# Convolution-fed attention: nine batches of eight key blocks instead of twelve of six

## The chip, the cores and the metric

The kernel runs on one core of one Trainium2 chip. The metric is device time in microseconds (us), the median of the runs shown. TensorE is called PE, its weight loads PEld, VectorE DVE, ScalarE ACT, GpSimd POOL, SyncE SP.

## The reference

The input x has shape (4, 384, 48, 48): four images, 384 channels, 2304 positions. All is fp32.

```
local  = depthwise_conv7x7(x) with batch norm
x_norm = layernorm(x over channels)
q, k, v = split(x_norm @ qkv_w.T + qkv_b)         # 8 heads of 48
q      = q + layernorm(local over channels)
attn   = softmax(q k^T * 48**-0.5)                # 2304 x 2304 per head
out    = x + (attn v) @ proj_w.T + proj_b
```

## The kernel before

An image has five groups of queries, of 8, 10, 10, 10 and 10 rows of 48 positions (`ROWS`), so 384 columns in the first group and 480 in the others. Four images make 20 groups, `t` = 0 to 19; `g` is the group's place in its image. Between images lies a stage that makes keys, values and raw queries out of the normalized x (`from_x`, six pieces), and adds up the output of the image before.

Within a group the attention loops over four pairs of heads and 18 blocks of 128 keys, 72 blocks in all. They are cut into 12 batches ("slots") of `BATCH` = 6 blocks. For one block `score` issues six matmuls (three terms for each of two heads, the heads on different halves of the array's rows) into a PSUM tile of two banks, one for each head, and one exponential on ACT over both heads (L1113), which writes a `pt` tile (four buffers). `score_batch` does this for six blocks. `weigh_batch` then multiplies the six `pt` tiles with the values (L1120), adding up in one more PSUM tile, `o`. So PE alternates: 36 score matmuls, then 12 weighing matmuls (each fp32 one is two records in the profile). PSUM is one ring of four tiles of two banks, tag `r`; the scores, the sums `o` and all other matmuls take their tiles from it in turn. A tile is free again when the engine that reads it is done.

A pair's sums come in three parts. ACT copies the first into its place in `ao` (L1007) and the others into `part_o` (L997, two buffers); DVE adds these (`sums_add`, L1016). The fourth pair has its own tile `aot`.

The order of each engine's work is written out by hand; each engine takes its instructions in that order. In slot s come: the scores; the first half of the slot's share of convolution on DVE (`convolve`, L340); `sums_add`; the weighing; the second half of the convolution. The share of each half is planned from `spare`, a hand-made table of DVE time left over. Around these lie steps that belong to the next group: the norm of its local convolution, in steps that are seven slots long, and, in late groups of an image, the norm of a piece of the next image's x. Groups 0 to 3 make the means of the query norm on PE (`early`). Groups 4 to 19 add up on DVE, send sums through DRAM by SP (`out`), and take a root of a small tile on ACT (`few_root`). `norm_slots` and `X_SLOTS` give the slots of these steps. `query_end` finishes the next group's queries; `high_queries` (ACT, L968) and `low_queries` (DVE, L973, and six DMAs on SP) split them into two parts and stack them in a `qs` tile for each head pair. `gather_tails` gathers by eight DMAs on SP the fourth pair's rows into `qt`. `load_keys` loads a third of a pair's keys (18 blocks are three thirds) from DRAM by POOL's queue into one of three `ks` buffers. `divide`, `hold` and `fetch` work on the output of the group before.

Of the kernel before, what the change touches and what calls it, by code (L numbers as in the profile page):

```python
# [16 lines left out]
P = 128  # L17
# [8 lines left out]
BATCH = 6  # L26
NSLOT = 12
X_SLOTS = 4, 7
X_LATER = 3
OUT_SLOT = 7  # L30
# [18 lines left out]
def unshifted_pass(  # L49
# [47 lines left out]
    ps = ctx.enter_context(tc.tile_pool(name="ps", bufs=4, space=bass.MemoryType.PSUM))  # L97
# [8 lines left out]
    def two_banks(name="r"):  # L106
        return ps.tile([P, 2, 512], F32, tag="r", name=name)
# [62 lines left out]
    third = BATCH * P  # L170
# [68 lines left out]
    def pack():  # L239
        m = two_banks()[:, 0, 0 : CC * (T0 + 1)].rearrange("p (c v) -> p c v", c=CC)  # L240
        for c in range(CC):
            mine = [pair for pair in pairs if pair[0] == c]
            for pair in mine:
                nc.tensor.matmul(
                    m[:, c, :],
                    lhsT=packing[:, pairs.index(pair), :],
                    rhs=natural[:, pair[1], :],
                    start=pair == mine[0],
                    stop=pair == mine[-1],
                )  # L250
        nc.scalar.copy(vec, m)
# [126 lines left out]
    def taps_out():  # L378
        m = two_banks()[:, 0, 0 : 4 * T0].rearrange("p (q v) -> p q v", q=4)
# [25 lines left out]
    def products():  # L405
        total = two_banks()[:, 0, : columns_of(1)]
# [21 lines left out]
    def norm_slots(t):  # L428
        return (8 - (t > 0), None) if t + 1 < NA else (5, 8)

    def spare(t, s, half):
        b, g = divmod(t, NA)
        first, second = norm_slots(t)
        time = 3.6 - (0.0 if half else 0.6) - (0.6 if half and s % 3 == 1 else 0.0)
        if b + 1 < B and g >= begins(b + 1):
            time -= {(2, 1): 2.3, (4, 1): 2.2, (5, 1): 2.3, (7, 0): 0.4, (8, 0): 2.6}.get(
                (s, half), 0.0
            )
        if g:
            time -= {(2, 0): 0.7, (7, 1): 1.4}.get((s, half), 0.0)  # L440
        if t + 1 < NA:
            if t:
                time -= {
                    (first, 0): 1.3,
                    (first + 1, 0): 1.4,
                    (first + 1, 1): 1.3,
                    (first + 2, 1): 4.3,
                    (first + 3, 1): 0.6,
                }.get((s, half), 0.0)
            else:  # L450
                time -= {(first + 1, 0): 1.4, (first + 2, 0): 4.3, (first + 2, 1): 0.6}.get(
                    (s, half), 0.0
                )
        elif g < NA - 1:
            time -= {
                (3, 1): 2.3, (5, 0): 1.2, (5, 1): 2.2, (6, 1): 2.3, (8, 0): 0.4, (8, 1): 1.5,
                (9, 0): 4.5,
            }.get((s, half), 0.0)
        return max(0.3, time) * columns_of(t) / G
# [21 lines left out]
    for t in range(NT):  # L481
# [3 lines left out]
        points += [("slot", t, s, h) for s in range(NSLOT) for h in range(2)]  # L485
        room += [spare(t, s, h) for s in range(NSLOT) for h in range(2)]
# [4 lines left out]
    for t in range(1, NT):  # L491
        last = ("slot", t - 1, norm_slots(t - 1)[0] - (t >= NA), t < NA) if t % NA else ("kv", t, 4, 0)
# [41 lines left out]
    class Norm:  # L534
# [41 lines left out]
        def mean_by_chunk(self, src, m=None):  # L576
            self.m = two_banks()[:, 0, : self.n] if m is None else m
            project(self.m, lambda c: mean_w, lambda c: src[:, c, :])
# [5 lines left out]
        def mean_kept(self, src):  # L584

            m = two_banks()[:, 0, : self.n]
# [3 lines left out]
        def mean_of_sum(self):  # L590

            m = two_banks()[:, 0, : self.n]
# [3 lines left out]
        def mean_in_place(self):  # L596

            self.m = two_banks()[:, 0, : self.n]
            nc.tensor.matmul(self.m, lhsT=mean_w, rhs=self.buf[:, 0, :], start=True, stop=True)

        def mean_of(self, src, at):

            self.m = two_banks()[:, 0, :G]
# [92 lines left out]
    def gather_tails(dst, src):  # L696

        for i, c in enumerate((*range(CC), 0)):
# [69 lines left out]
    def from_x(b, g, before=None, ao=None):  # L768
# [22 lines left out]
        def key(u, r):  # L791
# [7 lines left out]
            else:  # L799
                k = work.tile([P, 2, GM], HALF, tag="pt", name=f"k{b}_{g}_{u}", bufs=4)[:, :, :G]  # L800
# [33 lines left out]
        while todo:  # L834
            r = two_banks()
            steps = [f(i, r[:, j, :]) for j, (f, i) in enumerate(todo[:2])]
# [27 lines left out]
    def shift_rows():  # L864
        r = two_banks()
        for c in range(CC):
            for i in range(3):
                nc.tensor.matmul(
                    r[of_row(i), 0, :C],
# [5 lines left out]
        rows.update((i, r[of_row(i), 0, :C]) for i in range(3))  # L875
# [12 lines left out]
    def columns():  # L888

        r, r2 = two_banks(), two_banks()  # L890
        m = {1: r[:, 0, 0:CC], 2: r[:, 1, 0:CC], 0: r2[:, 0, 0:CC]}
# [9 lines left out]
        return m, r2[:, 1, :G]  # L901
# [22 lines left out]
    def output_bias():  # L924

        m = two_banks()[:, 0, 0:CC]
# [17 lines left out]
    def query_end(t, at_once=False):  # L944
# [3 lines left out]
        q3 = work.tile([P, GM], F32, tag="qt", name=f"qt{t}", bufs=1)[:, : columns_of(t)]  # L948
        queries[t] = q, q3
# [36 lines left out]
    ended = []  # L986
    parts_of = deque()

    def sums_out():

        if not ended:
            return
        t, p, i, sums = ended.pop()
        n = columns_of(t)
        if i:
            part = work.tile([P, GM], F32, tag="part_o", name=f"o{t}_{p}_{i}")[:, :n]
            nc.scalar.copy(part[0 : 64 + HA], sums[0 : 64 + HA, 0, :n])  # L997
            parts_of.append((t, p, i, part))
            return
        if p == 0:  # L1000
            ao = work.tile([P, CC, GM], F32, tag="ao", name=f"ao{t}")[:, :, :n]
            ao3 = work.tile([P, GM], F32, tag="aot", name=f"aot{t}", bufs=1)[:, :n]
            den = dram.tile([NH, n], F32, tag=f"den{n}", name=f"den{t}")
            outputs[t] = ao, ao3, den
        ao, ao3, den = outputs[t]
        dst = ao[:, p, :] if p < CC else ao3
        nc.scalar.copy(dst[0 : 64 + HA], sums[0 : 64 + HA, 0, :n])  # L1007

    def sums_add():
# [3 lines left out]
        t, p, i, part = parts_of.popleft()  # L1013
        ao, ao3, den = outputs[t]
        dst = (ao[:, p, :] if p < CC else ao3)[0 : 64 + HA]
        nc.vector.tensor_add(dst, dst, part[0 : 64 + HA])  # L1016
        if i < KB // BATCH - 1:
# [77 lines left out]
    jobs, between = deque(), deque()  # L1095
    weighing = deque()

    def score(t, p, kb):
        ks, qs = stacks[t // NA, p, kb // BATCH], stacked[t, p]
        at = slice(kb % BATCH * P, (kb % BATCH + 1) * P)  # L1100
        n = columns_of(t)
        r = two_banks()
        for i, (w, m) in enumerate(((0, 0), (0, 1), (1, 2))):
            for j, rows in enumerate(halves):
                nc.tensor.matmul(  # L1105
                    r[:, j, :n],
# [5 lines left out]
        pt = work.tile([P, 2, GM], F32, tag="pt", name="pt", bufs=4)[:, :, :n]  # L1112
        nc.scalar.activation(pt, r[:, :, :n], AF.Exp, scale=SCALE)  # L1113
        weighing.append((t, p, kb, pt))

    def weigh(i, sums):
        t, p, kb, pt = weighing.popleft()
        for j in range(2):
            first = (kb % NB * NH + 2 * p + j) * HA
            nc.tensor.matmul(  # L1120
                sums[halves[j], 0, : columns_of(t)],
                lhsT=values[t // NA, kb // NB][:, first : first + 64],
                rhs=pt[:, j, :],
                start=i == 0,
                stop=i == BATCH - 1,
            )

    def score_batch(t, s):
        p, k0 = s // (KB // BATCH), s % (KB // BATCH) * BATCH
        for kb in range(k0, k0 + BATCH):  # L1130
            score(t, p, kb)
            if between:
                between.popleft()()

    def weigh_batch(t, s):
        p, i = s // (KB // BATCH), s % (KB // BATCH)
# [4 lines left out]
        sums = two_banks("o")  # L1141
        for n in range(BATCH):
            weigh(n, sums)
        ended.append((t, p, i, sums))
        sums_out()
# [14 lines left out]
    def warm(n):  # L1160
        m = two_banks()[:, 0, 0:P]
# [31 lines left out]
    m, bank = columns()  # L1193
    convolve_first(10)
    norm = Norm(xn[0, 1])
    norm.mean_by_chunk(norm.src, bank)
# [88 lines left out]

    for t in range(NT):
# [73 lines left out]
        first, second = norm_slots(t)  # L1360
        for s in range(NSLOT):
            pair, part = divmod(s, KB // BATCH)
            score_batch(t, s)
            if part == 0 and pair < NP - 1:
                high_queries(t, pair + 1)
            if s == 0:
                gather_tails(*reversed(queries[t]))
            if s == 0 and g == 0:
                keep_stack(b, 2)
            if (s or g) and (s < NSLOT - 2 or g < NA - 1):  # L1370
                load_keys(b, s + 2, nc.scalar if g == 0 and s < 3 else nc.gpsimd)
            if s == 2 and g:
                rb = divide(t - 1)
            if s == 0 and coming:
                load_x(b + 1, g - begins(b + 1))
            if s == NSLOT - 4 and g == NA - 1:
# [4 lines left out]
                else:  # L1381
                    places = [("acc", 3)] * 3 + [("sq", 2)] * 2 + [("qs", 5)]
                    aos = []
                    for i in range(NG):
                        load_residual(b, i, *places[i])
                        aos.append(fetch(b, i) if i < NG - 1 else outputs[t][0])
            if coming and s == X_SLOTS[1] + 1:
                norm_x.scale(norm_x.few_newton())
            if following and s == second + 1:
                local_end(t + 1, norm.few_newton())  # L1390
                query_end(t + 1, True)
            if coming and s == X_SLOTS[0] + 1:
                jobs.extend(norm_x.square_jobs())
            if following and s == first + 1:
                jobs.extend(norm.square_jobs())
            if coming and s == X_SLOTS[1]:
                norm_x.few_variance()
            if following and s == second:
                norm.few_variance()
# [3 lines left out]
            else:  # L1403
                convolve("slot", t, s, 0)
            sums_add()
            if early and s == first + 1:
# [7 lines left out]
            if coming and s == X_SLOTS[1]:  # L1414
                norm_x.few_root()
            if following and s == second:
                norm.few_root()
# [3 lines left out]
            weigh_batch(t, s)  # L1421
            if early and s == first:
# [5 lines left out]
            if early and s == first + (2 if t == 0 else 3):  # L1428
                low_queries(t + 1, 0)
            convolve("slot", t, s, 1)  # L1430
            if t and early and s == first + 2:
# [589 lines left out]
```

## Time and profile before

| | |
|---|---|
| median of 3 runs | 2739.45 us (2737.72 to 2742.43) |
| the profiled execution | 2739.04 us |
| its span, first to last instruction | 2737.2 us, granted clock 0.997 |
| PE busy | 2714.7 us (99%) |
| DVE busy | 2314.8 us (85%) |
| ACT busy | 1671.1 us (61%) |
| POOL busy | 603.9 us (22%) |

The rows of a group name the line, the engine, the operation, what is written and read, and the shape; then come the number of instructions, the time in which at least one of them ran, the mean length of one in ns, and the idle time of the engine just before them with what ended it. Two matmuls that run side by side each have a record, so the mean length times the number is more than the busy time. In a timeline a row begins with its start and its length in us.

### The profile page before, as it was taken

To read this page: it belongs to the slowest core of one execution; us is meant where nothing else is said; L and a number is where in the kernel's file an instruction comes from. 1 tells how busy PE (TensorE), PEld (TensorE's weight loads), DVE (VectorE), ACT (ScalarE), POOL (GpSimd) and SP (SyncE) were. 2 spreads that over 40 slices of the span, in tenths; PEclk is the share of its full clock that TensorE was granted. 3 is DMA by queue.
4 is the path that set the end of the run, shared out by engine and by line. 5 is a ranking of instruction groups with operands and counts; after the bars stand their busy time and mean duration, and the time that the engine had idled before them with its cause. 6 is when DMAs were issued, how large, how long until landed. Compare 5 with 4: busy or idle time off the path is not lost.

```text
span 2737.2 us, 46047 instructions
## 1 busy us (share of the span) xinstructions
PE 2714.7 (99%) x16438; PEld 1536.6 (56%) x16438; DVE 2314.8 (85%) x4038; ACT 1671.1 (61%) x2317; POOL 603.9 (22%) x1077
## 2 busy tenths in 40 slices
PE   8999999999999999999999999999999999999999
PEld 5565555555556555555555655555555565555555
DVE  7999999989999999989889999889888998986212
ACT  4356777777325777777622677777752377776762
POOL 5541101102453111011155211111225511110110
PEclk9999999999999999999999999999999999999999
DMA  8354544446465545354555553545635544444442
GB/s 164 85 143 136 142 115 129 124 136 182 101 160 154 139 120 146 115 152 124 143 140 138 166 147 110 142 126 141 152 105 158 147 140 133 139 132 132 139 150 68
DMA packets 160223, 370.46 MB, mean 135 GB/s; under 512 B 58672, under 2 KB 107472, under 8 KB 159984
## 3 DMA queue, kind: packets, MB, share of 16 engines
q0 software_dynamic: 71424, 279.04, 35.6%
q1 hardware_dynamic: 83248, 78.33, 12.6%
q10 hardware_dynamic: 5312, 10.06, 1.1%
q8 instruction: 132, 2.16, 0.3%
q14 instruction: 107, 0.88, 0.1%
HBM read 258.14 MB, written 64.14 MB: 118 GB/s over the span
## 4 chain that ended last, share of the span: by engine, by line
PE 90%; DVE 5%; DMA 4%; ACT 0%; issue 0%; SPq 0%; POOL 0%; DVEq 0%; POOLq 0%; ACTq 0%
PE o L1120 42%; PE r L1105 34%; PE r L694 13%; DVE acc L340 2%; DMA parts<-part 1%; DMA staged<-in_qkv_wT_dram 1%; DVE k L804 0%; DMA slab<-in_x_dram 0%; PE r L415 0%; DMA four<-parts 0%; DVE xn L689 0%; DMA wide<-k 0%; DMA xn<-in_x_dram 0%; DMA out_dram<-xr 0%; DVE xr L1086 0%
## 5 line engine op out<-in xcount | busy, mean ns | idle before, releaser
L340 DVE SCALAR_TENSOR_TENSOR acc<-slab,vec,acc 128x470 f32<-128x470 f32 (+10 forms) x2832 | 1658.1, 658 | 2.0 <-ACT acc L303 2.0
L1113 ACT ACTIVATE pt<-r 128x960 f32<-128x960 f32 (+1 forms) x1440 | 1248.6, 943 | 246.4 <-PE o L1120 151.8
L1120 PE MATMUL o<-pt,v 128*64 128x480 f32 (+1 forms) x5760 | 1166.2, 554 | 0.4 <-ACT pt L1113 0.4
L1105 PE MATMUL r<-qs,ks 64*128 64x480 f32 (+1 forms) x8640 | 967.0, 373 | 4.8 <-ACT xn L818 3.0
L1105 PEld LDWEIGHTS r<-qs,ks 64*128 64x128 f32 x8640 | 785.2, 184 | 268.2 <-issue 171.6
L1120 PEld LDWEIGHTS o<-pt,v 128*64 128x64 f32 x5760 | 392.5, 137 | 659.9 <-issue 566.5
L766 POOL DMA_DIRECT2D ks<-wide x220 | 160.0, 727 | 1369.7 <-PE r L1105 1310.0
L694 PE MATMUL r<-xn,w_qk 128*128 128x384 f32 x864 | 284.7, 487 | 0.0
L997 ACT COPY o<-o 113x480 f32<-113x480 f32 (+1 forms) x160 | 87.1, 544 | 277.3 <-PE o L1120 276.7
L694 PEld LDWEIGHTS r<-xn,w_qk 128*128 128x128 f32 x864 | 164.4, 191 | 115.3 <-issue 1.8
L694 PE MATMUL r<-w_v,xn 128*128 128x384 f32 x432 | 145.3, 489 | 2.8 <-DVE xn L689 1.4
L788 ACT COPY v<-r 128x384 f32<-128x384 f32 x72 | 32.0, 479 | 183.3 <-PE r L694 183.3
L1016 DVE TENSOR_TENSOR ao<-ao,o 113x480 f32<-113x480 f32 (+1 forms) x120 | 75.9, 633 | 73.9 <-ACT o L997 73.9
L694 PEld LDWEIGHTS r<-w_v,xn 128*128 128x128 f32 x432 | 81.1, 190 | 62.6 <-DVE xn L689 3.8
L973 DVE TENSOR_TENSOR qs<-xn,qs 128x480 fp32r<-128x480 f32 (+1 forms) x60 | 38.1, 635 | 63.8 <-ACT qs L968 63.8
L751 POOL DMA_DIRECT2D wide<-k x144 | 72.4, 505 | 78.3 <-ACT k L801 64.2
L694 PE MATMUL r<-af,w_o 128*128 128x384 f32 (+1 forms) x270 | 85.2, 470 | 0.0
L1007 ACT COPY ao<-o 113x480 f32<-113x480 f32 (+1 forms) x60 | 32.6, 544 | 72.1 <-PE o L1120 72.1
L1016 DVE TENSOR_TENSOR aot<-aot,o 113x480 f32<-113x480 f32 (+1 forms) x40 | 25.4, 634 | 56.9 <-ACT o L997 56.9
L818 ACT ACTIVATE xn<-r,qkb 128x384 f32<-128x384 f32 x72 | 39.6, 576 | 50.8 <-PE r L694 47.6
L1086 DVE SCALAR_TENSOR_TENSOR xr<-r,pb,xr 128x384 f32<-128x384 f32 (+2 forms) x72 | 42.0, 611 | 33.2 <-PE r L694 26.0
L694 PEld LDWEIGHTS r<-af,w_o 128*128 128x128 f32 x270 | 51.3, 190 | 31.9
(148 smaller groups left out, 1354.9 us busy)
## 6 DMA issues: line engine op xcount, KB each, us to landing
ks<-wide POOLq DMA_DIRECT2D x220, 768.0 KB, 4.9
qs<-qs SPq DMA_DIRECT2D x352, 60.0 KB
slab<-in_x_dram POOLq DMA_DIRECT2D x24, 432.0 KB, 7.2
wide<-k POOLq DMA_DIRECT2D x96, 96.0 KB, 2.2
wide<-ks POOLq DMA_DIRECT2D x12, 768.0 KB, 5.3
xr<-in_x_dram POOLq DMA_DIRECT2D x16, 576.0 KB, 5.6
rb<-rden SPq DMA_DIRECT2D x32, 270.0 KB
held<-ao POOLq DMA_DIRECT2D x12, 720.0 KB, 3.9
```

The costliest lines, as they stand in the source:

```text
L340: nc.vector.scalar_tensor_tensor(dst, src, weight, dst, ALU.mult, ALU.add)
L694: nc.tensor.matmul(dst, lhsT=weights(c), rhs=src(c), start=c == 0, stop=c == CC - 1)
L751: nc.gpsimd.dma_start(out=last[16 * u : 16 * u + 16, 0], in_=k[r : r + 16, 0])
L766: queue.dma_start(out=place_keys(b, p, i), in_=wide[b, p][:, :, at])
L818: nc.scalar.activation(src[:, i, :], q[:, :G], AF.Identity, bias=qkb[:, 0, i : i + 1])
L973: nc.vector.tensor_sub(qs[:, 1, :], query_of(t, p), qs[:, 0, :])
L997: nc.scalar.copy(part[0 : 64 + HA], sums[0 : 64 + HA, 0, :n])
L1016: nc.vector.tensor_add(dst, dst, part[0 : 64 + HA])
L1086: nc.vector.scalar_tensor_tensor(xr[:, co, :], m, pb[:, co : co + 1], xr[:, co, :], ALU.add, ALU.add)
L1105: nc.tensor.matmul(r[:, j, :n], lhsT=ks[rows, w, at], rhs=qs[rows, m, :], start=i == 0, stop=i == 2,)
L1113: nc.scalar.activation(pt, r[:, :, :n], AF.Exp, scale=SCALE)
L1120: nc.tensor.matmul(sums[halves[j], 0, : columns_of(t)], lhsT=values[t // NA, kb // NB][:, first : first + 64], rhs=pt[:, j, :], start=i == ...
```

## The change

Groups 4 to 19 have nine batches of eight blocks; groups 0 to 3 keep twelve of six. A batch of eight can cross from one head pair to the next; then its weighing has two sums. PSUM is a ring of eight single banks, tag `r`: a block takes one for each head, the sums take one. Each head has its own exponential. `pt` has five buffers instead of four (the key tiles that share the tag also); `part_o` has one instead of two; the fourth pair's output uses the tag of the gathered tails (`qt`) instead of its own. The steps of the norms, of the division and of the queries have new places, given as (slot, stage) in tables: stage 0 lies between the scores and the first half of the convolution, 1 before the weighing, 2 before the second half of the convolution, 3 after it. Some ACT steps (`few_root`, and `high_queries` of the next group) are put in a queue `in_gap`, which is emptied among the scores, after the block that is fourth from the batch's end (the fifth of eight). The other pairs' queries are split in slots 0, 2, 4 instead of 0, 3, 6. `gather_tails` is issued after `sums_add` instead of before it. The planner's table `spare` is new for nine slots.

```diff
-BATCH = 6
-NSLOT = 12
-X_SLOTS = 4, 7
+THIRD = 6
+PLACES_9 = {
+    "x_sum": (1, 3), "x_centre": (3, 1), "x_squares": (3, 1), "x_sum_squares": (3, 3),
+    "x_variance": (4, 3), "x_root": (4, 3), "x_scale": (5, 3),
+    "divide": (1, 1), "multiply": (5, 1), "fetch": (6, 0),
+    "q_sum": (2, 3), "q_centre": (4, 1), "q_squares": (4, 1), "q_sum_squares": (4, 3),
+    "q_variance": (5, 3), "q_root": (5, 3), "q_end": (6, 1), "q_high": (6, 3), "q_low": (7, 3),
+}
+HIGHS = {12: (0, 3, 6), 9: (0, 2, 4)}
...
-    ps = ctx.enter_context(tc.tile_pool(name="ps", bufs=4, space=bass.MemoryType.PSUM))
+    ps = ctx.enter_context(tc.tile_pool(name="ps", bufs=8, space=bass.MemoryType.PSUM))
...
-    def two_banks(name="r"):
-        return ps.tile([P, 2, 512], F32, tag="r", name=name)
+    def bank(name="r"):
+        return ps.tile([P, 512], F32, tag="r", name=name)
...
+    def few_slots(t):
+        return t + 1 >= NA
+
+    def n_slots(t):
+        return 9 if few_slots(t) else 12
+
+    def batch(t):
+        return NP * KB // n_slots(t)
...
+        if few_slots(t):
+            time = 4.7 if half else 4.0
...
     def score(t, p, kb):
...
-        r = two_banks()
+        r = bank(), bank()
         for i, (w, m) in enumerate(((0, 0), (0, 1), (1, 2))):
             for j, rows in enumerate(halves):
                 nc.tensor.matmul(
-                    r[:, j, :n],
+                    r[j][:, :n],
...
-        pt = work.tile([P, 2, GM], F32, tag="pt", name="pt", bufs=4)[:, :, :n]
-        nc.scalar.activation(pt, r[:, :, :n], AF.Exp, scale=SCALE)
+        pt = work.tile([P, 2, GM], F32, tag="pt", name="pt", bufs=5)[:, :, :n]
+        for j in range(2):
+            nc.scalar.activation(pt[:, j, :], r[j][:, :n], AF.Exp, scale=SCALE)
         weighing.append((t, p, kb, pt))
...
     def score_batch(t, s):
-        p, k0 = s // (KB // BATCH), s % (KB // BATCH) * BATCH
-        for kb in range(k0, k0 + BATCH):
-            score(t, p, kb)
+        n = batch(t)
+        for i in range(n):
+            score(t, *divmod(s * n + i, KB))
             if between:
                 between.popleft()()
+            while i == n - 4 and in_gap:
+                in_gap.popleft()()
 
     def weigh_batch(t, s):
...
-        sums = two_banks("o")
-        for n in range(BATCH):
-            weigh(n, sums)
-        ended.append((t, p, i, sums))
-        sums_out()
+        i = s * n
+        while i < (s + 1) * n:
+            p, first = divmod(i, KB)
+            many = min(KB - first, (s + 1) * n - i)
+            sums = bank("o")
+            for k in range(many):
+                weigh(k == 0, k == many - 1, sums)
+            sums_out(t, p, first == 0, first + many == KB, sums)
+            i += many
...
+        for s in range(n_slots(t)):
             score_batch(t, s)
...
+            if few_slots(t):
+                n = batch(t)
+                if t == NA - 1 and s == 0:
+                    load_keys(b, 2)
+                for i in range(s * n // THIRD, (s + 1) * n // THIRD):
+                    if i + 3 < NP * 3 or g < NA - 1:
+                        load_keys(b, i + 3)
...
             sums_add()
+            if s == 0:
+                gather_tails(t)
```

## The prediction

> **What bounds the kernel now.** First the page's busy times, to see which engine has no slack.
>
> ```profile
> PE 2714.7 (99%) x16438; PEld 1536.6 (56%) x16438; DVE 2314.8 (85%) x4038; ACT 1671.1 (61%) x2317; POOL 603.9 (22%) x1077
> ```
>
> TensorE (PE) is busy 2714.7 of 2737.2 us, so what saves no PE time and adds no PE wait is worth nothing. Next, groups of instructions with shapes kept apart: the score matmuls (L1105), the weighing matmuls (L1120) and the exponentials (L1113).
>
> ```profile
> L1113 ACT ACTIVATE pt<-r 128x960 f32<-128x960 f32 x1152 | 1035.4, 974 | 192.8 <-PE o L1120 127.2 <-PE r L1105 65.1
> L1120 PE MATMUL o<-pt,v 128*64 128x480 f32 x4608 | 969.8, 570 | 0.0
> L1105 PE MATMUL r<-qs,ks 64*128 64x480 f32 x6912 | 800.2, 381 | 0.9 <-DMA qs<-qs 0.9
> L1113 ACT ACTIVATE pt<-r 128x768 f32<-128x768 f32 x288 | 213.2, 815 | 53.6 <-PE o L1120 24.6 <-DMA wide<-k 15.3 <-PE r L1105 13.3
> ```
>
> Before the matmuls PE was idle 0.9 us in all: today it waits for nobody in the attention. Third, the timeline of one batch on PE, then on ScalarE (ACT).
>
> ```profile
> 1003.76 4.17 PE L1105 MATMUL r<-qs,ks 64*128 64x480 f32 x36
> 1007.86 5.05 PE L1120 MATMUL o<-pt,v 128*64 128x480 f32 x24
> 1012.84 1.34 PE L1105 MATMUL r<-qs,ks 64*128 64x480 f32 x10
> ```
>
> ```profile
> 1003.88 0.56 ACT L997 COPY o<-o 113x480 f32<-113x480 f32 x1 [2.13 <-PE o L1120]
> 1004.78 3.56 ACT L1113 ACTIVATE pt<-r 128x960 f32<-128x960 f32 x4 [0.34 <-PE r L1105]
> 1008.99 1.83 ACT L1113 ACTIVATE pt<-r 128x960 f32<-128x960 f32 x2 [0.66 <-PE o L1120]
> ```
>
> A batch lasts 1012.84 - 1003.76 = 9.08 us. In its single records matmuls start in pairs (two heads side by side): score pairs every 0.217 us, but 0.320 from the first to the second; 0.312 from the last score pair to the first weighing pair; weighing pairs every 0.4025, but 0.453 after the first and 0.503 from the last to the next batch's scores. So 9.08 = 6 x (3 x 0.217 + 2 x 0.4025) + fixed cost, and each batch has a **fixed cost** of 0.103 + 0.095 + 0.050 + 0.100 = 0.348 us. Tiles of 384 columns (steps 0.175 and 0.323) give 0.350.
>
> On ACT four exponentials run back to back (3.56 = 3 x 0.863 + 0.97); the fifth waits for the first weighing, to free one of four `pt` buffers. ACT then idles 1.5 to 2 us per batch: it is not the bound, but it is the pacemaker of PSUM's release.
>
> **Fewer batches (gain).** Sixteen of the 20 groups go from 12 batches to 9: 16 x 3 = 48 batches fewer, 48 x 0.348 = 16.7 us off the path. Matmuls stay the same in number. Where a batch crosses a head pair (batches 2, 4, 6) the weighing changes its bank once; a change of bank between score blocks costs nothing (0.217 on both sides), so 0.
>
> **Eight scores at a stretch (loss).** With eight banks, two per block, the scores of block k need the banks of block k-4: blocks 4, 5, 6, 7 wait for the exponentials of 0, 1, 2, 3. Before, a batch had only blocks 4 and 5, and exponentials 0 and 1 were done early. Now ACT, slower per block than PE (0.85 against 0.651), is raced for two blocks more.
>
> The price of a 480-column exponential is not in the trace. The single records give the spacing back to back: 0.850 for 960 elements, 0.690 for 768, hence 0.833 ns per element plus 0.050 us, so 0.450 per head at 480, **0.900 per block against 0.850**. The nearest rows at 480: the PSUM copies of L997 (0.560 long; a record outlasts its spacing by 0.121, so 0.439) and the SBUF casts of L968 (0.593, spaced 0.480). I take 0.450, from the same operation, source and line; ends 0.439 and 0.480.
>
> The Trainium skill, ScalarE: Activation LUTs, What ACT_TABLE_LOAD costs, says that an ACTIVATE with immediates takes 186 ns + 0.833 ns per element and that neighbours overlap by 93 ns. By that rule a block would go from 893 to 986 ns; this trace's 850 at 960 elements is below it. With 0.493 per head the sum below would be about +71 us, the span about 2808.
>
> Now the race, from the batch's first score. Exponential 0 starts at 1.017 (the trace: 1004.78 - 1003.76); the first spacing is 0.019 longer; a record outlasts its spacing by 0.121; PE starts 0.053 after ACT's end where it really waited (an exponential ended at 245.829 us, the score load started at 245.880). After that wait the next step was 0.278 instead of 0.175: 0.103 of restart, as the load is otherwise issued a pair ahead. Bounds of the restart: 0 (a load 0.10 late cost 0.04) and 0.103; I take 0.103.
> - Block 6 would start at 0.103 + 18 x 0.217 = 4.010; its banks and restart allow 1.017 + 0.019 + 6 x 0.450 + 0.121 + 0.053 + 0.103 = 4.013. No wait.
> - Block 7 would start at 0.103 + 21 x 0.217 = 4.661; allowed 4.913. **Wait 0.25 us.**
> - 384 columns: exponential 0 at 0.895 (median of those batches), head spacing 0.370. Block 7 would start at 3.78, allowed 1.017 + 0.019 - 0.122 + 8 x 0.370 + 0.277 = 4.15. Wait 0.37.
>
> Per group of 480: 9 x 0.25 - 3 x 0.348 = +1.2 us, 13 groups: +15.7. Per group of 384 (the first of images 1 to 3): 9 x 0.37 - 1.05 = +2.3, three: +6.9. **Sum +22.6 us.** With the cheap ends (0.439, restart 0) the same lines give -0.5 x 13 + 0.6 x 3 = -4.7; with 0.480 and restart 0.103, +57.
>
> **The rest of the batch.** The fifth `pt` lets exponential 4 run among the scores; 5, 6, 7 wait for weighings 0, 1, 2 and end about 9.6 us into a batch of 12.2, when weighing 7 needs its own at 11.3: no wait. ACT's 2.6 us up to the next batch hide the query copies (0.59) or squares (1.5). The four first groups keep batches of six, never reach blocks 6 and 7, and pay the dearer exponential on ACT's slack: 0. Without that slack it would be 0.05 x 72 = 3.6 us a group.
>
> **Norm steps and queues.** DVE has the same number of kinds of work, 85% busy, 102.32 of 108.90 us in a full group (below). The root of the query norm now sits in ACT's gap after exponential 4 of batch 6, 5.6 us in, while DVE reaches the steps that need it some 2 us in: DVE idles about 4 us there in 12 groups. Cover: 6.58 us idle in this group already.
>
> ```profile
> 1040.10:1149.00 108.90, 108.90 (x724) 59.16 (x722) 102.32 (x176) 79.11 (x103) 13.87 (x21) 1.00 0.48 132
> ```
>
> The subtraction for the next group's first queries (L973) ran 18.6 us before the group began (1130.4 against 1149.0). Now it comes after batch 7's second half; walking DVE's order with these durations, about 3 us into batch 8, 9 us before. Its six DMAs on SP are issued within 3.2 us, and land some 2 later: 4 us to spare. The tails' gather goes behind the last sum's DMAs on SP, but is read only in batch 4, over 40 us later. Key thirds on POOL are freed at least 15 us before use, and land in 4.9. The single `part_o` is refilled at the earliest 7 us into a batch, when DVE is normally past the sum before it. All taken at 0. The key and value stages (three of 140 us, PE without a gap), start and end keep their order: 0.
>
> **Sum.** Span 2737.2 + 22.6 = 2759.8; the execution took 2739.04, 1.84 more than its span: 2761.6. The median 2739.45 lies 0.4 above that execution, so 2762.
>
> **Rivals.**
> - *Faster: the banks come in time.* Place: block 7's first pair. Price: 9 x wait per group against 1.04 saved; it decides at a wait of 0.116, that is a head spacing of 0.433 with the full restart, or 0.446 without. At no wait all 16.7 us arrive: 2723. For it: copies from PSUM extrapolate to 0.439, and the restart rests on one case. Against: both widths of the exponential itself give 0.050 of overhead. With the cheap ends it is 2735, within the "same" band or just beyond.
> - *Much slower: the next group's queries come late.* If DVE falls over 4 us further behind (its subtraction later than about 7 us into batch 8), PE waits one for one at 12 group starts; 3 us each is +36, on top of the forecast 2798. For it: reserve shrinks from 13 us to 4, and the idle in some groups of image 1 is only 3 to 5 us. Against: PE's own waits give DVE 1 to 2 us more per group. The same place on the axis is reached with 0.480 per head.
> - *Same:* a wait near 0.12, 2735 to 2745.
>
> **Chances.** A run of this kernel can be told from no change by about 0.2%, 5.5 us. Forecast (2745 to 2782) 0.53; much slower 0.17; same 0.10; faster (below 2734) 0.20. Forecast and much slower make 0.70 slower. For 8 in 10 I go from 2730 (leaving half of the faster case out) to 2794 (the +57 of the dear end, and most of the late queries). The forecast's own range is 2745 to 2782.
>
> **What would show it.** Right: on the timeline the scores of a full batch last about 5.7 us instead of the 5.5 that eight blocks need (8 x 0.651 + 0.20 of fixed cost + the last record's tail), with a pause at block 7 that the exponentials end; batches of 12.25 us, groups of 110.2; exponentials 0.57 us long, spaced 0.45; the next queries' subtraction 9 us ahead. Wrong: no pause and batches of 12.0 (first rival), or PE idle until a `qs` DMA at group starts (second).

## The result, and the profile after

| | before | after |
|---|---|---|
| median of the runs | 2739.15 us (6 runs) | 2824.52 us (6 runs, 2820.21 to 2831.77) |
| ratio | 1 | 1.0311, 95% interval 1.0295 to 1.0327 |
| span of the profiled execution | 2737.2 us | 2820.7 us, granted clock 0.991 |

The change costs 85 us, 3.1%. The forecast was 2762, with a range up to 2794: the sign was right, the size not. The page of after begins with the busy times; further down, the shares by engine of the chain that ended last:

```profile
PE 2768.9 (98%) x16438; PEld 1582.4 (56%) x16438; DVE 2310.6 (82%) x4038; ACT 1752.2 (62%) x3757; POOL 605.6 (21%) x1083
...
PE 71%; DVE 13%; DMA 7%; issue 4%; SPq 3%; ACT 1%; POOL 0%; ACTq 0%; DVEq 0%; POOLq 0%
```

PE is "busy" 54 us longer for the same matmuls, and for 52 us it is not busy at all (before: 22). The chain leaves PE for 29% of the span, to DVE, DMAs and SP's queue. The groups, with shapes kept apart, and last the row of the reciprocal from the page:

```profile
L1149 ACT ACTIVATE pt<-r 128x480 f32<-128x480 f32 x2304 | 1098.7, 605 | 191.2 <-PE o L1156 124.7 <-PE r L1140 66.0
L1156 PE MATMUL o<-pt,v 128*64 128x480 f32 x4608 | 964.5, 570 | 5.4 <-ACT pt L1149 5.4
L1140 PE MATMUL r<-qs,ks 64*128 64x480 f32 x6912 | 848.0, 389 | 30.2 <-DMA qs<-qs 23.8 <-ACT o L1042 6.4
...
L1077 DVE RECIPROCAL rd<-rd 128x30 f32<-128x30 f32 (+1 forms) x20 | 6.7, 333 | 153.6 <-DMA rd<-den 153.6
```

Three things are new. The score matmuls are busy 47.8 us longer (800.2 before): much of that is the pause at the end of each stretch of eight, too short for the record to call it idle. They also sit idle 30.2 us, where before it was 0.9, and the DMA that brings a split query (`qs<-qs`) ends most of it. And DVE waits 153.6 us for the DMA that brings the sums to be inverted (`rd<-den`; before 23.4).

From the single records of the matmuls come the lengths of the groups. Group 0 is the first; groups 5, 10 and 15 have 384 columns. A group that nothing disturbs takes 110.8 us instead of 108.9 (91.15 instead of 88.7). Nine groups take over 1 us longer than that: 6 (120.5), 7 (118.4), 8 (116.3), 9 (114.4), 11 (114.1), 12 (118.3), 13 (112.1), 14 (116.4) and 16 (121.0). So there are two losses. The **steady** one is 13 x 1.87 + 3 x 2.5 = 32 us. The **stalls**, what groups 4 to 19 take above their undisturbed length, are 55 us. Together that is more than the 83.5 us by which the span grew: in this execution the start and the stages between the images took some 6 us less than before, groups 0 to 3 2.5 us more.

**The steady loss.** PE, then ACT, in a batch of group 17:

```profile
2459.88 5.80 PE L1140 MATMUL r<-qs,ks 64*128 64x480 f32 x48
2465.61 6.66 PE L1156 MATMUL o<-pt,v 128*64 128x480 f32 x32
2472.20 3.97 PE L1140 MATMUL r<-qs,ks 64*128 64x480 f32 x34
```

```profile
2460.89 4.74 ACT L1149 ACTIVATE pt<-r 128x480 f32<-128x480 f32 x10 [0.30 <-PE r L1140]
2466.74 2.88 ACT L1149 ACTIVATE pt<-r 128x480 f32<-128x480 f32 x6 [1.11 <-PE o L1156]
```

The scores take 2465.61 - 2459.88 = 5.73 us; eight blocks unhindered need 5.41. The pause is at block 7, and ten exponentials (five `pt` tiles, two heads each) run without a gap from 1.01 us after the batch's first score to 5.75. So PE is held by ACT, at the place that was forecast, by 0.32 us instead of 0.25.

**The stalls.** The second head pair begins in batch 2, at its third block. In group 7 (1055.2 to 1173.6) PE waits there. PE, then SP's queue:

```profile
1079.86 1.57 PE L1140 MATMUL r<-qs,ks 64*128 64x480 f32 x12
1084.24 0.46 PE L1140 MATMUL r<-qs,ks 64*128 64x480 f32 x1 [2.82 <-DMA qs<-qs]
...
1087.36 5.95 PE L1140 MATMUL r<-qs,ks 64*128 64x480 f32 x31 [1.67 <-DMA qs<-qs]
```

```profile
1065.35 0.52 SPq L1056 DMA_DIRECT2D den<-aot  x2
1065.91 3.67 SPq L1060 DMA_DIRECT2D ao<-aot  x6
1071.13 4.93 SPq L736 DMA_DIRECT2D qt<-xn  x8
1077.41 0.51 SPq L1011 DMA_DIRECT2D qs<-qs  x1
...
1081.79 1.25 SPq L1013 DMA_DIRECT2D qs<-qs  x2
1083.35 0.35 SPq L1067 DMA_DIRECT2D rd<-den  x1
```

These are issues on SP, in order. The last sum's row is sent off (`den`), the fourth pair's output is copied to its place (`ao<-aot`, six DMAs), and then comes the tails' gather (`qt<-xn`). It writes the tile that the copies read. So it begins only 1.55 us after the last of them was issued, when they have landed, and its eight issues take 4.93 us. Behind it stand the six DMAs of the second pair's queries (`qs`) and the load of the sums (`rd`). Before, in the same group, these DMAs began 11.2 us after the group's first score (1051.27 - 1040.10). Now it is 22.2 (1077.41 - 1055.2), and PE stops for them at 26.2, where its twelfth record ends (1079.86 + 1.57). SP in the kernel before, then DVE in after, where it splits these queries:

```profile
1051.27 0.51 SPq L978 DMA_DIRECT2D qs<-qs  x1
```

```profile
1070.67 0.65 DVE L1006 TENSOR_TENSOR qs<-xn,qs 128x480 fp32r<-128x480 f32 x1
```

Not all of these 11 us are the gather's. DVE begins the split 15.5 us into the group (1070.67 - 1055.2); before, it was 10.5. From its end, at 1071.32, the DMAs wait another 6.1 us for their turn on SP.

DVE is stopped by the `rd` behind them, ACT by DVE, PE by ACT. In group 6 that chain reads, on DVE, on ACT and on PE:

```profile
967.77 0.30 DVE L1077 RECIPROCAL rd<-rd 128x24 f32<-128x24 f32 x1 [12.79 <-DMA rd<-den]
...
979.61 0.65 DVE L1051 TENSOR_TENSOR ao<-ao,o 113x480 f32<-113x480 f32 x1
```

```profile
980.29 0.56 ACT L1042 COPY o<-o 113x480 f32<-113x480 f32 x1 [7.57 <-DVE ao L1051]
```

```profile
980.91 3.63 PE L1140 MATMUL r<-qs,ks 64*128 64x480 f32 x15 [3.85 <-ACT o L1042]
```

DVE loses 12.79 us at the reciprocal, comes late to the sum of the first pair, and holds the only `part_o` tile until then. ACT's next copy waits 7.57 us for that tile, with the exponentials behind it in ACT's order.

A stall costs more than its idle time. These are stretches of 2 us around batch 2 of group 16: length, busy time of PE, PEld, DVE, ACT and POOL, granted clock, DMA share, GB/s.

```profile
2356.00:2358.00 2.00, 0.00 (x0) 0.00 (x0) 0.00 (x0) 0.00 (x0) 0.00 (x0) 0.50 0.94 310
2362.00:2364.00 2.00, 2.00 (x12) 1.66 (x10) 1.94 (x5) 1.51 (x4) 0.00 (x0) 0.50 0.05 6
2366.00:2368.00 2.00, 2.00 (x17) 1.08 (x15) 2.00 (x5) 0.00 (x0) 0.49 (x1) 1.00 0.79 146
```

PE had two waits here, of 1.40 and 6.44 us, with one matmul between. The clock falls to 0.50 and stays there until 2365.4, 4.4 us after PE began again at 2361.05. Until then score pairs start 0.400 us apart instead of 0.217. So the batch's scores are 10.2 us longer: 7.84 of idle, about 2 of half speed. Short waits do it too: at the start of group 11 PE waited 1.69 us, the clock was 0.50 for 3.41 us, and the batch took 3.4 us longer. In the clock records of this trace each stretch at 0.50 lasts 3.41, 6.83 or 10.24 us, but for the one that the span's end cuts off. The Trainium skill, TensorE: Matmul & The Clock Gate, Part 1, has the clock at half rate after one idle window of some 3.4 us and at full rate after one busy window. Here the rise, after 4.4 us, agrees with that; the fall came sooner: the clock's mean was 0.79 from 2354 to 2356, so it fell at 2355.2, some 2.4 us after the scores first stopped at 2352.77, and one matmul ran in between. The sums above don't need the rule.

### The profile page after: what moved, and what is told of

Same layout as the page of the kernel before. It is cut to its first block, busy times and chain, and to the rows that moved or that the text cites. A ratio compares the mean times of both kernels' runs of the same rounds, so it can differ in the third digit from the quotient of the medians.

```text
span 2820.7 us, 47356 instructions
## 1 busy us (share of the span) xinstructions
PE 2768.9 (98%) x16438; PEld 1582.4 (56%) x16438; DVE 2310.6 (82%) x4038; ACT 1752.2 (62%) x3757; POOL 605.6 (21%) x1083
## 4 chain that ended last, share of the span: by engine, by line
PE 71%; DVE 13%; DMA 7%; issue 4%; SPq 3%; ACT 1%; POOL 0%; ACTq 0%; DVEq 0%; POOLq 0%
PE o L1156 28%; PE r L1140 25%; PE r L727 18%; DVE acc L350 10%; DMA qs<-qs 1%; DMA ao<-aot 1%; SPq L736 1%; DMA parts<-part 1%; DMA ks<-wide 1%; ACT pt L1149 1%; SPq L1060 1%; DMA four<-parts 1%; DMA qt<-xn 1%; SPq L1013 1%; DMA staged<-in_qkv_wT_dram 0%
## 5 line engine op out<-in xcount | busy, mean ns | idle before, releaser
L1149 ACT ACTIVATE pt<-r 128x480 f32<-128x480 f32 (+1 forms) x2880 | 1327.2, 589 | 246.0 <-PE o L1156 147.9
L1140 PE MATMUL r<-qs,ks 64*128 64x480 f32 (+1 forms) x8640 | 1023.7, 380 | 33.3 <-DMA qs<-qs 26.8
L1140 PEld LDWEIGHTS r<-qs,ks 64*128 64x128 f32 x8640 | 825.8, 187 | 296.0 <-issue 149.9
L1077 DVE RECIPROCAL rd<-rd 128x30 f32<-128x30 f32 (+1 forms) x20 | 6.7, 333 | 153.6 <-DMA rd<-den 153.6
L837 ACT ACTIVATE k<-r,qkb 128x384 fp32r<-128x384 f32 x72 | 41.2, 580 | 68.9 <-PE r L727 62.5
L124 POOL DMA_DIRECT2D slab<-in_x_dram x76 | 42.0, 558 | 161.9 <-DVE acc L350 155.2
```

The source lines that it names most:

```text
L124: queue.dma_start(out=dst[p0 : p0 + piece.shape[0]], in_=piece)
L837: nc.scalar.activation(k[:, 0, :], r[:, :G], AF.Identity, bias=bias)
L1140: nc.tensor.matmul(r[j][:, :n], lhsT=ks[rows, w, at], rhs=qs[rows, m, :], start=i == 0, stop=i == 2,)
L1149: nc.scalar.activation(pt[:, j, :], r[j][:, :n], AF.Exp, scale=SCALE)
```

## The experiments

"After" and "before" below are the two kernels; a ratio is to before, with its 95% interval. The first question: is it SP's queue, or DVE's division in its new place, that makes the stalls?

**1. The gather behind the division** (e1_gather_behind). In after, the gather goes to batch 1, behind the division's DMAs (batch 2 in groups 0 to 3).

```diff
             sums_add()
-            if s == 0:
-                gather_tails(t)
...
             steps()
+            if s == (1 if few_slots(t) else 2):
+                gather_tails(t)
```

> The changed kernel with one thing moved: the tails' gather (eight DMAs on SP) is issued in batch 1 (batch 2 where there are twelve) after the division's DMAs, no longer in batch 0 right after the sum. Theory A (SP's order): the gather waits for the copies out of the buffer it shares, and holds up behind it the next pair's query DMAs and the load of the denominators, for which DVE then idles. Then PE's idle time on query DMAs falls from 26.8 us to under 3, DVE's idle time before the reciprocal from 153.6 to under 40, and every group of 480 takes about 110.7 us, as groups 17 and 18 do now: 2824.5 - 56 - 3 = about 2766 us (2758 to 2776). Theory B (the new places of the norm steps, or the single part buffer, overload DVE): DVE's idle time moves to another wait and the time stays above 2800.

Measured: 2776.73 us (2774.30 to 2779.32), 1.0129 [1.0112, 1.0146]. **48 us of the 85 are the place of these eight DMAs.** PE's idle time for `qs` falls from 26.8 to 10.2 us, DVE's wait for `rd` from 153.6 to 73.0. Both fall less than theory A asked, and the time lies just above its range. In group 7, which here begins at 1048.45, DVE splits the second pair's queries as late as in after, but their DMAs follow at once:

```profile
1063.91 0.64 DVE L1006 TENSOR_TENSOR qs<-xn,qs 128x480 fp32r<-128x480 f32 x1
```

```profile
1064.61 0.51 SPq L1011 DMA_DIRECT2D qs<-qs  x1
```

They begin 16.2 us into the group (1064.61 - 1048.45), against 22.2 in after and 11.2 before. So 6 of the 11 us are the gather, and 5 are DVE.

The undisturbed groups keep 110.8. Left are groups 6 (112.9), 7 (116.4), 11 (112.3) and 13 (111.6): 10 us.

**2. The division one batch later** (e2_divide_later), the gather left where the change put it.

```diff
-    "divide": (1, 1), "multiply": (5, 1), "fetch": (6, 0),
+    "divide": (2, 1), "multiply": (5, 1), "fetch": (6, 0),
```

> The changed kernel with the division one batch later in the groups of nine batches (slot 2, stage 1). The gather stays where it is. Theory A splits the loss in two: query DMAs late at the second pair (some 27 us of PE waits in batch 2), and DVE idle before the reciprocal, which makes ACT wait in order for DVE (some 27 us in batches 3 to 5). Then DVE's idle time before the reciprocal falls under 40 us, the waits in batch 2 stay, and the time is about 2795 us (2785 to 2808). If all came from late query DMAs, it stays at 2824; if all came from DVE's idle time, it falls to about 2768.

Measured: 2807.96 us (2804.91 to 2815.88), 1.0254 [1.0235, 1.0273]. 16.6 us come back, at the upper end of what was expected. DVE's wait for `rd` falls to 36.5 us, and the stalls in batches 3 to 5, those by way of DVE, are gone but for 2 us in group 8. Those in batch 2 stay, the scores lasting 12.4 to 15.6 us in groups 6, 7, 12 and 16, with 29.4 us of PE idle for `qs`. So DVE's wait and the late queries are two effects of one queue.

**3. Only the exponentials by head, in the kernel before** (e3_by_head). This tells the dearer exponential from the longer batch.

```diff
-        nc.scalar.activation(pt, r[:, :, :n], AF.Exp, scale=SCALE)
+        for j in range(2):
+            nc.scalar.activation(pt[:, j, :], r[:, j, :n], AF.Exp, scale=SCALE)
```

> The kernel before with nothing changed but two exponentials per block, one for each head, out of the same PSUM tile of two banks. Theory: with six blocks a batch PE needs only exponentials 0 and 1 among the scores, and those come early enough; ACT's longer work (0.90 to 0.93 us a block instead of 0.85 to 0.87) hides. 2739 us, within 5. Rival: the two records per block cost PE time by themselves (semaphores, PSUM); then about 0.05 us x 1440 = 72 us more, 2811.

Measured: 2738.15 us (10 runs), 0.9992 [0.9983, 1.0002]: ACT busy 1760.7 us instead of 1671.1, the groups 108.9 as before. In batches of six the 90 us more on ACT cost nothing.

**4. Two banks and one exponential a block** (e4_two_banks), in experiment 1's kernel. Four PSUM tiles of two banks; a batch that crosses a head pair takes two of them for its sums. Two of the edits:

```diff
-        r = bank(), bank()
+        r = two_banks()
...
-        for j in range(2):
-            nc.scalar.activation(pt[:, j, :], r[j][:, :n], AF.Exp, scale=SCALE)
+        nc.scalar.activation(pt, r[:, :, :n], AF.Exp, scale=SCALE)
```

> As e1_gather_behind, but with PSUM as four tiles of two banks again and one exponential for both heads of a block; batches of eight stay. A batch that crosses a head pair takes two such tiles for its sums. Theory (a race between scores and exponentials): block 7 waits for exponential 3, which now ends at 1.017 + 0.867 + 0.851 + 0.850 + 0.992 = 4.58 us instead of 4.82, so the wait falls from 0.32 to about 0.07 us a batch; the second sums of batch 2 wait some 0.5 us for exponential 5. Groups of 480: 9 x 12.07 + 0.5 = 109.1 us instead of 110.7, of 384: 89.4 instead of 91.2; 13 x 1.6 + 3 x 1.8 = 26 us less than e1_gather_behind, about 2740 (2732 to 2750). Rival (the pause at block 7 belongs to the matmuls or to the switch to weighing, not to the exponentials): the same as e1_gather_behind.

Measured: 2765.09 us (2759.41 to 2769.29), 1.0089 [1.0071, 1.0106]. The scores take 5.50 us, a wait of 0.09, and the groups 109.3 and 89.7, near what was expected. So the steady loss depends on when the exponentials end, as the theory has it. The expected total was missed by 25 us: group 11 now takes 118.0, groups 6 and 7 112.7 and 114.2.

**5. Exponentials of half the length** (e5_short_exp), in experiment 1's kernel. Each exponential is taken over half of its columns and used twice, so part of the computation is left out. It takes the race away and keeps PE's matmuls; ACT is busy 1306.1 us instead of 1751.4.

```diff
-            nc.scalar.activation(pt[:, j, :], r[j][:, :n], AF.Exp, scale=SCALE)
+            nc.scalar.activation(pt[:, j, : n // 2], r[j][:, : n // 2], AF.Exp, scale=SCALE)
...
-                rhs=pt[:, j, :],
+                rhs=pt[:, j : j + 1, : columns_of(t) // 2].to_broadcast([P, 2, columns_of(t) // 2]),
```

> As e1_gather_behind, but each exponential takes only the first half of its columns, and the weighing uses that half twice, so that the matmuls keep their shapes (the second half of the queries gets the first half's weights). Theory (race): with exponentials 0.25 us apart nothing waits at block 7; the scores of a batch of 480 take 5.41 us instead of 5.73, a batch 12.0, a group 108.0 us, below the 108.9 of the kernel before: the saving of fewer batches is real and shows. Groups of 384: 87.5 instead of 91.2. Total 13 x 2.8 + 3 x 3.7 = 47 us below e1_gather_behind's 2777, about 2730 (2722 to 2738). Rival (the longer score stretch costs PE by itself): scores stay near 5.7 and the time above 2765.

Measured: 2735.58 us (10 runs), 0.9987 [0.9977, 0.9997]. In this kernel a batch has no pause:

```profile
2479.75 5.47 PE L1140 MATMUL r<-qs,ks 64*128 64x480 f32 x48
2485.15 6.66 PE L1156 MATMUL o<-pt,v 128*64 128x480 f32 x32
2491.74 5.47 PE L1140 MATMUL r<-qs,ks 64*128 64x480 f32 x48
```

A batch lasts 2491.74 - 2479.75 = 11.99 us and an undisturbed group 107.93 (87.47 for 384 columns), against 108.90 (88.7) before. **The saving of three batches a group is real, 0.97 us, and the race takes 110.80 - 107.93 = 2.87 us of it back**, that is 9 x 0.32. The total shows little of the saving, since stalls stay here too: groups 6, 7, 8 and 11 (111.6, 112.5, 109.4 and 117.0) are together 18.7 us above 107.93.

**6, 7, 8. The last 10 us, by a new order.** Experiment 6 (e6_gather_and_divide) is 1 with the division of 2 and the gather in batch 2. Experiment 7 (e8_root_early) takes the root of the query norm at once in batch 5, instead of in ACT's gap. Experiment 8 (e7_two_banks_laid_out) is 7 with two banks.

```diff
-    "divide": (1, 1), "multiply": (5, 1), "fetch": (6, 0),
+    "divide": (2, 1), "multiply": (5, 1), "fetch": (6, 0),
...
-    "q_variance": (5, 3), "q_root": (5, 3), "q_end": (6, 1),
+    "q_variance": (5, 1), "q_root": (5, 1), "q_end": (6, 1),
...
-                in_gap.append(norm.few_root)
+                norm.few_root()
...
-            if s == 0:
-                gather_tails(t)
...
+            if s == 2:
+                gather_tails(t)
```

> e1_gather_behind with the division also one batch later (slot 2, stage 1), the gather after it in batch 2. Theory: what e1_gather_behind still loses beyond the race (about 13 us, at the starts of groups 6, 7, 11, 13 and in batch 2 of group 7) comes from DVE's 73 us of waits before the reciprocal. Then these fall under 20 us and the time to about 2766 (2760 to 2772). Rival: it comes from DVE's wait for the root in the gap of batch 6 (51 us): no change, 2777.

> e6_gather_and_divide with the query norm's variance and root in batch 5, stage 1, the root issued at once and not in the gap of batch 6. DVE's wait for that root (51 us) should fall under 25. If it is what still makes queries late, the time falls by what is left beyond the race, to about 2764; if DVE has the slack for it, nothing changes against e6_gather_and_divide.

> e8_root_early with four PSUM tiles of two banks and one exponential per block, as in e4_two_banks. Its groups stand at 109.3 and 89.8 us without other waits, against 108.9 and 88.7 before: 13 x 0.4 + 3 x 1.1 = 8.5 us. If all late queries are gone it takes about 2747 us (2742 to 2756): even the best form of nine batches tried here does not beat twelve. If queries stay late as in e4_two_banks, 2765.

Measured, in this order: 2783.18 us, 1.0163 [1.0146, 1.0180]; 2777.44 us, 1.0136 [1.0119, 1.0153]; 2765.55 us, 1.0104 [1.0081, 1.0126]. None is better than 1 or 4 by more than the runs scatter; the first is slower. In experiment 6 DVE's wait for `rd` is down to 6.5 us, and groups 6, 7, 11 and 13 take 5.5 us less than in experiment 1, but group 8 now stalls (120.2) on `qs` in its batch 4. It is the gather again, now ahead of the third pair's queries on SP:

```profile
1193.15 15.21 SPq L736 DMA_DIRECT2D qt<-xn  x8
```

Its eight issues take 15.21 us here, not 4.93, and the queries' first DMA leaves at 1208.45. In experiment 7 DVE's wait for the root falls from 56.6 to 4.8 us, but group 11 takes 116.2, in experiment 8 117.1. The totals forecast for 6 and 7 (2766 and 2764) fail. How much of the rest the wait for `rd` made isn't settled, since new stalls came with its end. Each new order moves the stalls to another group.

**9, 10. The two halves of the gather's cost, in the kernel before.** First the gather is only moved behind the sum's DMAs, with twelve batches and the old tiles. Then the fourth pair's output also shares the tails' tile.

```diff
-            if s == 0:
-                gather_tails(*reversed(queries[t]))
...
             sums_add()
+            if s == 0:
+                gather_tails(*reversed(queries[t]))
```

```diff
-            ao3 = work.tile([P, GM], F32, tag="aot", name=f"aot{t}", bufs=1)[:, :n]
...
+        if p == CC:
+            outputs[t][1] = work.tile([P, GM], F32, tag="qt", name=f"aot{t}", bufs=1)[:, :n]
```

> The kernel before, with the tails' gather issued behind the last sum's DMAs on SP, as the change has it, but with the fourth pair's output still in a tile of its own. Theory (the gather costs because it must wait for the copies out of the tile that it shares, and holds the queue meanwhile): here it has nothing to wait for, so 2739 us within 5. Rival (it is the order on the queue itself, 14 DMAs ahead of the queries): the second pair's queries come late in full groups, 2755 to 2790.

> The same, and the fourth pair's output in the tile of the gathered tails, as the change has it; still twelve batches, two part_o tiles and two banks. Theory (the shared tile makes SP's queue stand still, and whatever is behind it is late): the timeline of SP shows the gather some 5 us behind the last sum, and the time is 2750 to 2790, with PE idle for qs in some groups. Rival (the queue's stop only costs because DVE's order of nine batches has no reserve left at a group's start): below 2745.

Measured: 2746.72 us (8 runs), 1.0033 [1.0022, 1.0044], then 2759.71 us (2757.28 to 2770.56), 1.0073 [1.0056, 1.0090]. SP's queue in group 7, the first kernel and then the second:

```profile
1054.73 3.92 SPq L1025 DMA_DIRECT2D ao<-aot  x6
1058.69 5.01 SPq L700 DMA_DIRECT2D qt<-xn  x8
1063.80 0.53 SPq L978 DMA_DIRECT2D qs<-qs  x1
```

```profile
1062.88 3.67 SPq L1028 DMA_DIRECT2D ao<-aot  x6
1068.11 4.93 SPq L703 DMA_DIRECT2D qt<-xn  x8
1073.14 0.53 SPq L980 DMA_DIRECT2D qs<-qs  x1
```

With a tile of its own the gather follows the copies at once (1054.73 + 3.92 = 1058.65); sharing the tile, it stands still for 1.56 us. The order alone costs 7 us, so neither theory nor rival of experiment 9 gave its number; in the profiled execution groups 7 (114.8) and 2 (113.9) alone take over 1 us more than before. Sharing the tile costs some 13 us more, within the theory of experiment 10. Together they are 20 us in twelve batches, against 48 in nine. What is different there is seen in the sums' DMAs (`den`), which follow an addition on DVE: in groups 6 to 9 and 11 to 14 they leave 1.4 to 6.4 us after the group's first score before, 5.4 to 10.1 us after it in after and in experiment 1. So the same delay on SP starts from a later point. In experiments 9 and 10 too the largest stall lies where `den` leaves late: in group 7, at 10.3 and 10.0 us. That the later start makes 48 out of 20 is read from these times; no run with the gather in this place changed DVE's lateness alone.

**11, 12. Lighter DVE**, to see whether DVE makes the rest. Experiments 1 and 4, with each convolution of groups 5 to 19 over one row of positions fewer (that row is left out), some 7 us of DVE a group.

```diff
             else:
+                if t > 4 and dst.shape[1] > 1:
+                    dst, src = dst[:, :-1], src[:, :-1]
                 nc.vector.scalar_tensor_tensor(dst, src, weight, dst, ALU.mult, ALU.add)
```

> e1_gather_behind with the convolution of groups 5 to 19 over one row of positions fewer in each operation (that row's part of the result is left out), so that DVE has some 7 us less to do in each group; nothing else moves. Theory (what is left of the stalls is DVE being late with the next queries): groups 6 to 16 all take 110.8 us (91.2 for 384 columns), some 10 us off e1_gather_behind: 2766. Rival (it is the order of the queues or of PSUM's ring, whatever DVE does): groups 6, 7, 11 and 13 stay above 111.5 and the time stays at 2774 to 2779.

> e4_two_banks with the same lighter convolution. Theory (DVE late, as above, hid what two banks give): groups of 109.3 and 89.8 throughout, group 11 too, so 17 to 19 us off e4_two_banks: 2747. Rival: group 11 stays near 118 and the time at 2760 to 2769.

Measured: 2772.63 us, 1.0114 [1.0097, 1.0131], and 2757.86 us (2755.38 to 2758.93), 1.0059 [1.0042, 1.0076]. Both totals lie between theory and rival. In the first kernel groups 7 and 13 are cured (111.1 and 110.7): DVE's share of the rest is shown there. Group 6 still takes 111.8, and group 11, at 116.4, is worse than in experiment 1. In the second, group 11 takes 116.0 and group 6 113.3. In the first kernel group 11 begins at 1609.39. SP's queue, POOL's queue, PE, and stretches of 4 us (as above, the last three columns being clock, DMA share and GB/s):

```profile
1602.04 0.55 SPq L1013 DMA_DIRECT2D qs<-qs  x1
...
1604.54 1.23 SPq L1015 DMA_DIRECT2D qs<-qs  x2
```

```profile
1603.97 1.12 POOL L124 DMA_DIRECT2D slab<-in_x_dram  x2 [11.37 <-DVE acc L352]
1605.08 0.74 POOL L804 DMA_DIRECT2D ks<-wide  x1
```

```profile
1614.25 6.56 PE L1142 MATMUL r<-qs,ks 64*128 64x480 f32 x43 [3.95 <-DMA qs<-qs]
```

```profile
1604.00:1608.00 4.00, 4.00 (x25) 1.78 (x26) 4.00 (x8) 2.48 (x7) 3.65 (x6) 1.00 0.75 162
1608.00:1612.00 4.00, 2.30 (x15) 0.91 (x11) 4.00 (x9) 1.05 (x2) 0.00 (x0) 1.00 1.02 263
```

The queries' DMAs are all issued by 1605.77, 3.6 us before they are needed, but PE goes on at 1614.25, 8.5 us after the last issue. Meanwhile POOL has started the next image slab and two thirds of keys, and the DMA engines are full from 1608 on. The slab's load waits for DVE to finish the convolution that reads it. It starts 1.8 us before the queries' last issue ends; before, in this group, it started 3.1 us after it, and PE waited for nothing. In experiment 1 it starts 1.6 us before it, and PE waited only 1.11 us, so this order alone doesn't give the length of the wait. The Trainium skill, DMA: Bandwidth & Descriptors, Issuing engines are not separate DMA queues, says that DMAs started by different engines run on the same 16 engines and interleave. The share of 1.02, with SP's and POOL's transfers both under way, agrees with that. That the slab is what delayed these queries is read from the coincidence; a kernel with the slab's load moved wasn't tried.

## Why the prediction was wrong

**What bounds the kernel: right.** Only PE's time counted: experiment 3 put 90 us on ACT and the time didn't move.

**Fewer batches: right.** Forecast 0.348 us a batch, 1.04 a group; experiment 5 shows 0.97, and 13 x 0.97 + 3 x 1.15 = 16.1 us for the forecast 16.7.

**Eight scores at a stretch: the right place, a term that was mis-sized.** The spacing of the exponentials was right: their starts are 0.451 us apart, 0.450 forecast. The wrong term is the 0.121 by which a record outlasts its spacing, taken as a constant. In this run of ten the records grow, 0.572 for the first and 0.637 for the eighth, whose end frees block 7's bank. So that end comes 1.012 + 0.019 + 7 x 0.451 + 0.637 = 4.82 us into the batch, not 4.757. The wait is 0.32 instead of 0.25 us, the steady loss 32 instead of 22.6.

For the rule on ScalarE that the prediction weighed: 0.493 a head is not what ACT does here, 0.451 is. That its total, 2808, lies nearer to the result is chance.

**Norm steps and queues: the step that failed.** "The tails' gather goes behind the last sum's DMAs on SP, but is read only in batch 4, over 40 us later", so 0: that looked at who reads the gathered tile, not at what stands behind the gather in its queue. Neither did it see that the tile is the one the copies just ahead are still reading. The wait of 1.55 us and eight issues of 0.6 us delayed the second pair's queries and the sums' load by some 6 us, and this cost 48 us where 0 was forecast (experiment 1). Why it cost so much is read from the times and not from a run of its own: the reserve was smaller too. DVE splits the second pair's queries 5 us later than before in group 7, which the prediction didn't work out, and the two add up to the 11 us there.

**The single `part_o`: taken at 0, and it did cost, but only as a consequence.** ACT waited 36.9 us for it, 7.57 in the row above. It costs where DVE is behind: with the division moved, the wait fell to 15.5 us (experiment 2), with the gather moved to 8.5 (experiment 1). Undoing the single tile by itself wasn't tried.

**The next queries: half right.** "9 us before" the group is what the trace shows in full groups (8.8 to 10.7). In groups 6, 11 and 16, which follow the short group, it is 6.1 to 7.0, which was not worked out. And "land some 2 later" fails wherever other transfers run: 8.5 us in the row above. The much slower rival, the next group's queries late, is thus seen at the starts of groups 6 and 11, for 4.8 us in after (with 2.8 us of idle). The start of group 11 is late in every kernel of nine batches tried here, by 1.4 to 9.0 us. "PE waits one for one" was too cheap, since the clock falls as well.

**DVE's 4 us at the root: about as forecast.** In after DVE waited for `few_u` 15 times, 51.1 us in all (before 11 times, 17.1 us). Taking the root early brought 6 us (2783.18 to 2777.44), with intervals that meet: not settled.

The terms measured, -16 and +48 for the steady part (13 x 2.87 + 3 x 3.68), 48 for the gather, 10 for the rest, add up to 90, not 85. They come from different executions, in which group 0 starts at 160.2 to 164.4 us. What stays open is which order of nine batches would have no late query. The best one that computes everything (experiment 4) is 0.9% slower than before. Without a race (experiment 5), but with the stalls that stay, nine batches gain 0.13%.

## What to carry to other kernels

When a DMA is moved, read the queue, not its reader: list what stands behind it, what it must itself wait for (a shared tile makes a wait that the diff doesn't show), and when the first of those behind is needed. Before lengthening a stretch on the engine that bounds, lay out the rival engine's ends, not its starts. A margin of a few microseconds ahead of a transfer holds only while nothing else is moving: look up what the other queues start in that window.

## What the runs showed of the hardware

- Exponentials of 128x480 back to back start 0.451 us apart, but their records grow along a run, from 0.572 to 0.667 us over ten. What waits for an end pays for that.
- After a stall PE's clock was 0.50 for another 4.4 us: 7.84 us of idle cost 10.2. At the start of group 11 1.69 us of idle cost 3.4.
- Six DMAs of 60 KB released PE only 8.5 us after the last issue when the DMA engines were full (share 1.02, 263 GB/s).
